# Linear attention with memories and a mixture of experts: values and logits projected in the routing, sorting in small steps, one-hots beside four tiles

## The chip, the cores and the metric

The kernel runs on one core of a Trainium2 chip. The core has a matrix engine (TensorE, PE in the profile; its weight loads are shown apart as PEld), a vector engine (VectorE, DVE), a scalar engine (ScalarE, ACT), a general engine (GpSimd, POOL) and an engine that here only issues transfers (SyncE, SP). Each works through its own queue of instructions in order and waits on semaphores for the others. TensorE writes its results to PSUM, of which this kernel uses eight banks of 512 fp32 values in each of 128 partitions; DVE and ACT read them from there. The metric is the device time of one execution in microseconds (us), and less is better. "Before" is the kernel as found, "after" the changed one.

## What is computed

The input x has 4096 tokens (4 sequences of 1024) of 256 channels. It is layer-normalised, and the result xn goes through an attention layer and a feed-forward layer; both outputs are added to x. Cut to what matters:

```python
xn = layernorm(x)
# attention, 16 heads of 16
q, k, v = (split(xn @ w.T) for w in (w_q, w_k, w_v))
sq, sk = elu(q) + 1, elu(k) + 1
out_coarse = (sq @ M) / (sq @ z)                    # M, z: four memories summed
out_fine = sum_m w[m] * (sq @ memory[m]) / (sq @ norm[m])
gprob = sigmoid(relu(coarse_repr @ eg_w1.T + eg_b1) @ eg_w2.T + eg_b2)
memory_output = gprob * out_fine + (1 - gprob) * out_coarse
local_output = causal_linear_attention(q, k, v)      # chunks of 128 tokens, running state
attn = (gate * memory_output + (1 - gate) * local_output) @ w_o.T
# experts: 8, each token goes to its best 2
scores = softmax(xn @ gate_weight.T)
cw = normalised weights of the two largest scores, else 0
y = sum_e cw[e] * (silu(xn @ w_gate[e].T) * (xn @ w_up[e].T)) @ w_down[e].T
y += (silu(xn @ sw_gate.T) * (xn @ sw_up.T)) @ sw_down.T     # shared expert
out = x + attn + y
```

The weights w[m] are a softmax over the memories of the mean of sq @ norm[m] over a sequence, so a whole sequence's queries have to be known before its first memory output.

## The kernel before, in words

All arithmetic is fp32. Tokens are handled in 32 tiles of 128, and in 8 blocks of four tiles. Python lists of units, each with a weight, are merged in proportion (`mix`) or cut into parts of equal weight (`split`), and their functions are called in that order (`run`); the schedule is manual, so each engine's queue holds its instructions just as the functions are called. What decides the time is therefore where in the lists a unit stands, and on which buffers it has to wait.

*The routing.* For each block: x is loaded (`load_x`), DVE makes the statistics (`statistics`; POOL takes the inverse root for two blocks together), ACT and DVE normalise in place (`normalize`, three tiles on ACT, one on DVE), SP writes the normalised block to the array xns in DRAM, TensorE transposes it (`transpose_x`, L334, copied to xnT by ACT), and `logits` multiplies xnT with a 128-column strip of the joined weights wvg to get 8 logits a token (L348). Six blocks of x fit; blocks 6 and 7 are loaded into the buffers of 0 and 1 once those are written to xns. Route of the first half and the queries of the first two blocks (L550) stand between the last blocks.

*The sorting.* `route` finds each token's two largest logits, `sort` counts by a matmul with a triangle of ones (pp), `slots` turns the counts into places, `shift_logits` and `weights` make the weights of the chosen experts, `owners` says which expert owns which of 71 slots of 128 places. Each is a run of short DVE instructions. Then 22 batches of at most three one-hots (a batch covers three of 64 columns of choices) invert the list: `invert` makes the one-hots on DVE (L499, L503) and two products on POOL (held, L510), `add_slots` adds them up by matmul into one bank (found, L518). `inverted` reads the slots' tokens (islot) and weights from it. These steps are mixed with the first block's keys, values and shared expert and the first two attention rounds.

*Attention rounds.* A round (`attention_round`) takes one tile through scores (L658, into quad), masks (DVE, L665), memories (L770, quad again), weights of the memories (L780 to L785), fine parts (L799), local output (pn, L684), the way back (pb, L700 and L706, read by DVE L714 to L718), the running state (pu, L750) and, one and two tiles later, the gate (`gate_hidden` L830, `gate_out` L840) and the output (po). Beside the first 28 rounds run the projections of later blocks: keys, values (`values`, L578), queries, shared gate and up (L856, L871).

*Experts.* From round 2 to round 29 (`first_round`, `last_round`) the 71 slots are spread evenly: gather 128 tokens from xns (`fetch`, POOL; SP loads the owner's weights), transpose (pxg, L959), gate and up (phe, L968), transpose (pTe, L982), down (pye, L991), and an indirect transfer that adds to the array sums in DRAM (`put`, L1000). The last four rounds add the parts up and write the output.

*PSUM.* quad takes four banks for the whole kernel; every other matmul takes its bank from a ring of four (`bank`, pool ps_r). A bank is given out anew when its last reader is through, and which bank that is has been settled when the program is built.

Of the kernel before, what the change touches and what calls it, by code (L numbers as in the profile page):

```python
# [8 lines left out]
FP = mybir.dt.float32  # L9
# [5 lines left out]
P = 128  # L15
# [7 lines left out]
def linear_attention_moe_kernel(  # L23
# [51 lines left out]
    AHEAD = 6  # L75
# [10 lines left out]
    big = ctx.enter_context(tc.tile_pool(name="big", bufs=AHEAD))  # L86
# [3 lines left out]
    ps_q = ctx.enter_context(tc.tile_pool(name="ps_q", bufs=1, space=bass.MemoryType.PSUM))  # L90
# [6 lines left out]

    quad = ps_q.tile([P, NG, 512], FP, tag="quad", name="quad")

# [4 lines left out]
    def load_x(blk):  # L104
        xb = big.tile([P, NT, H], FP, tag="tok", name=f"x_{blk}", bufs=AHEAD)
        nc.sync.dma_start(
            xb, x[blk * TB : (blk + 1) * TB, :].rearrange("(n p) h -> p n h", p=P)
        )
        st["x", blk] = xb

    for blk in range(AHEAD):
        load_x(blk)
# [18 lines left out]
    b1 = const.tile([HID, 1], FP, tag="b1", name="b1")  # L131
    nc.scalar.dma_start(b1, eg_b1)
    w2 = const.tile([HID, 1], FP, tag="w2", name="w2")
    nc.scalar.dma_start(w2, eg_w2)
# [23 lines left out]
    neghalf = const.tile([P, 2, NT], FP, tag="neghalf", name="neghalf")  # L158
# [129 lines left out]
    def statistics(blk):  # L288

        xb = st["x", blk]  # L290
        if blk % 2 == 0:
            st["mv"] = small.tile([P, 2, NT, 2], FP, tag="mv", name=f"mv_{blk}", bufs=3)
            st["rstd"] = small.tile([P, 2, NT], FP, tag="rstd", name=f"rstd_{blk}", bufs=3)
        mv, rstd = st["mv"], st["rstd"]
        for i in range(NT):
            stats = small.tile([P, 6], FP, tag="stats", name=f"stats_{blk}_{i}")
            nc.vector.bn_stats(stats, xb[:, i, :])
            nc.vector.bn_aggr(mv[:, blk % 2, i, :], stats)
        if blk % 2:
            nc.vector.tensor_scalar(rstd, mv[:, :, :, 1], LN_EPS, None, ALU.add)  # L300
            nc.gpsimd.tensor_tensor(rstd, rstd, neghalf, ALU.pow)
        st["norm", blk] = mv[:, blk % 2], rstd[:, blk % 2]

    def normalize(blk):
# [9 lines left out]
        nc.vector.tensor_scalar(  # L314
            xb[:, NT - 1, :], xb[:, NT - 1, :], mv[:, NT - 1, 0:1], rstd[:, NT - 1 : NT],
            ALU.subtract, ALU.mult,
        )
        for i in range(NT - 1):
# [7 lines left out]
        if blk + AHEAD < NBLK:  # L326
            load_x(blk + AHEAD)

# [13 lines left out]
    def logits(blk):  # L342

        xnT = st["xnT", blk]
        pl = bank(f"pl_{blk}").rearrange("p (i e) -> p i e", i=NT)
        for i in range(NT):
            for k in range(NC):
                nc.tensor.matmul(  # L348
                    pl[:, i, :], xnT[:, k, i * P : (i + 1) * P], wvg[:, k, H + E - P : H + E],
                    start=(k == 0), stop=(k == NC - 1),  # L350
                )
        nc.scalar.copy(lgs[:, blk * NT : (blk + 1) * NT, :], pl[:, :, P - E :])

    def route(half):
# [12 lines left out]
        def first_largest(v, best, m, name):  # L367

            nc.vector.tensor_tensor(m, v, spread(best), ALU.is_equal)
            nc.vector.tensor_mul(m, m, first[:, None, :].to_broadcast(sh))  # L370
            at = t2(name + "_at")
            nc.vector.tensor_reduce(at, m, AX.X, ALU.max)
            nc.vector.tensor_tensor(m, m, spread(at), ALU.is_equal)

# [3 lines left out]
        first_largest(lg, best, m1, "m1")  # L378
# [4 lines left out]
        first_largest(rest, low, m2, "m2")  # L383
        st["best", half] = best

    def shift_logits():
# [8 lines left out]
        nc.scalar.activation(gatew, gatew, AF.Exp)  # L395

    def weights():
# [4 lines left out]
        nc.vector.reciprocal(tot, tot)  # L402
        nc.vector.tensor_mul(gatew, gatew, tot[:, :, None].to_broadcast(sh))
        two = st["two"]
        both = tmp.tile([P, 2, NTT, E], FP, tag="h", name="chosen", bufs=2 * NF)
        nc.vector.tensor_mul(both, picks, gatew[:, None].to_broadcast([P, 2, NTT, E]))
        nc.vector.tensor_reduce(two, both.rearrange("p r i e -> p (r i) e"), AX.X, ALU.add)
        nc.vector.tensor_add(tot, two[:, :NTT], two[:, NTT:])
# [3 lines left out]
        nc.vector.tensor_mul(t2, t2, tot[:, None, :].to_broadcast([P, 2, NTT]))  # L412

    def sort():
# [5 lines left out]
        nc.vector.tensor_add(both, pick[0], pick[1])  # L420
        pp = bank("pp").rearrange("p (w i e) -> p w i e", w=2, e=E)
# [5 lines left out]
        st["pp"] = pp  # L427

    def slots():
        work, pp = st.pop("work"), st.pop("pp")  # L430

        cnt = work[:, 1].rearrange("p (e i) u -> p e (i u)", e=E)
        nc.vector.tensor_copy(cnt, pp[:, 0].rearrange("p i e -> p e i"))
        upto = work[:, 2].rearrange("p (e i) u -> p e (i u)", e=E)
# [3 lines left out]
        )  # L438

# [12 lines left out]
        st["ends"] = ends  # L452
        nc.vector.tensor_sub(wholef, ends, wholef)
        nc.vector.tensor_sub(upto, upto, cnt)
        nc.vector.tensor_add(upto, upto, wholef[:, :, None].to_broadcast([P, E, NTT]))
        place = work[:, 3]
        nc.vector.tensor_add(place, pp[:, 1], upto.rearrange("p e i -> p i e"))
        both = work[:, 0:2]
        nc.vector.tensor_mul(both, picks, place[:, None].to_broadcast([P, 2, NTT, E]))
        slot = small.tile([P, 2 * NTT], FP, tag="slot", name="slot", bufs=1)  # L460
        nc.vector.tensor_reduce(slot, both.rearrange("p r i e -> p (r i) e"), AX.X, ALU.add)

# [6 lines left out]
        st["lohi"] = lohi  # L469

    def owners():
# [10 lines left out]
        )  # L482
        ownf = small.tile([P, NST], FP, tag="ownf", name="ownf", bufs=1)
        nc.vector.tensor_reduce(ownf, own_e, AX.X, ALU.add)
        nc.vector.tensor_scalar(owner, ownf, float(E - 1), float(F), ALU.min, ALU.mult)

    def invert(lo):
# [21 lines left out]
        for v, what in enumerate((token, two)):  # L509
            nc.gpsimd.tensor_mul(  # L510
                held[:, :, v], tiles, what[:, some, None].to_broadcast([P, n, NST])
            )
        st["one hot", lo] = places, held
# [23 lines left out]
    def project(blk, w, c, is_q):  # L537
# [18 lines left out]
        nc.scalar.activation(ex, ex, AF.Exp, scale=-1.0)  # L556
        if is_q:
            nc.vector.scalar_tensor_tensor(  # L558
                st[name, blk][:, c, :], pq, 0.0, ex, ALU.max, ALU.add,
                accum_out=st["qs", blk][:, c : c + 1],  # L560
            )
        else:
            nc.vector.scalar_tensor_tensor(  # L563
                st[name, blk][:, c, :], pq, 0.0, ex, ALU.max, ALU.add
            )

    def values(blk, i):
        xnT = st["xnT", blk]
        if i == 0:
            wide = att.tile([P, NT, NH * D1 + CW - D1], FP, tag="va", name=f"va_{blk}")  # L570
            nc.gpsimd.memset(wide[:, :, NH * D1 :], 0.0)
            va = wide[:, :, : NH * D1].rearrange("p i (h k) -> p i h k", k=D1)
            nc.gpsimd.memset(va[:, :, :, HD:D1], 1.0)
            st["va", blk] = va
            st["wide", blk] = wide
        pv = bank(f"pv_{blk}_{i}")
        for k in range(NC):
            nc.tensor.matmul(  # L578
                pv[:, :H], xnT[:, k, i * P : (i + 1) * P], wvg[:, k, :H],
                start=(k == 0), stop=(k == NC - 1),  # L580
            )
        nc.scalar.copy(
            st["va", blk][:, i, :, :HD],
            pv[:, :H].rearrange("p (h k) -> p h k", k=HD),
        )
# [623 lines left out]
```

## Time and profile before

| what | value |
|---|---|
| median of 3 runs | 777.4 us (773.6 to 777.79) |
| the profiled execution's own time | 782.79 us |
| its span (first to last instruction) | 781.1 us |
| busy in the span: PE, PEld, DVE, ACT, POOL | 700.7, 491.0, 426.1, 273.8, 400.3 us |
| last logits of the routing start | 55.8 us |
| first expert slot's transpose starts | 155.6 us |
| rounds 2, 4, 28 and 30 start (first scores) | 156.2, 201.3, 703.0, 733.0 us |
| mean granted TensorE clock | 0.956 of full |

Engines are busy side by side, so their times don't add up to the span. A group of instructions is written as line, engine, operation, output<-input by the program's names, shapes and count, then busy time, mean length in ns, the engine's idle time just before, and what ended that. In a list of waits stand the engine, its line, what it waited for, the sum in us, how often, and the longest. The line of 40 digits cuts the span into equal slices of 19.5 us and gives the busy share of each in tenths. Idle time of an engine counts only where nothing else is late.

### The profile page before, as it was taken

How to read it: one execution, taken by the hardware profiler on the slowest of the kernel's cores; microseconds unless marked ns; L12 is line 12 of the kernel's file. 1: busy time of each engine (PE TensorE's matmuls, PEld its weight loads, DVE VectorE, ACT ScalarE, POOL GpSimd, SP SyncE). 2: the span in 40 equal slices, each digit the busy share in tenths (PEclk: the TensorE clock that was granted, in tenths of full speed). 3: DMA queues.
4: the chain of work that ended last, by engine and by line, in shares of the span. 5: the costliest groups of instructions: out<-in, count | busy, mean ns of one | idle time of the engine just before them, and what ended most of it. 6: DMA issues, size and time to landing. Idle time of an engine off the chain costs nothing.

```text
span 781.1 us, 14630 instructions
## 1 busy us (share of the span) xinstructions
PE 700.7 (90%) x5268; PEld 491.0 (63%) x5268; DVE 426.1 (55%) x1084; ACT 273.8 (35%) x707; POOL 400.3 (51%) x441
## 2 busy tenths in 40 slices
PE   1798579499999999999999999999999999999965
PEld 0675356366676666666667667666766667767653
DVE  6536857445446744455536644554457555655553
ACT  2563002123443333433443343433443344334300
POOL 3100366506555656464546555556545646657576
PEclk9899689889999999999999999999999999999976
DMA  9554000234343453344444443443443444454285
GB/s 283 183 178 134 1 0 1 59 107 97 84 117 85 90 118 84 86 106 94 97 111 92 103 104 84 93 113 84 97 104 85 107 101 103 108 123 99 29 261 171
DMA packets 86373, 81.48 MB, mean 104 GB/s; under 512 B 7437, under 2 KB 83901, under 8 KB 86173
## 3 DMA queue, kind: packets, MB, share of 16 engines
q1 hardware_dynamic: 69661, 59.64, 26.5%
q0 software_dynamic: 13632, 18.62, 14.3%
q10 hardware_dynamic: 3008, 2.28, 0.9%
q8 instruction: 42, 0.69, 0.4%
q14 instruction: 30, 0.25, 0.1%
HBM read 62.56 MB, written 22.15 MB: 108 GB/s over the span
## 4 chain that ended last, share of the span: by engine, by line
PE 76%; DVE 7%; DMA 5%; POOL 4%; ACT 3%; issue 3%; SPq 0%; POOLq 0%; DVEq 0%; ACTq 0%
PE phe L968 12%; PE pye L991 8%; PE po L895 5%; PE psu L871 5%; PE pg L856 5%; PE quad L658 4%; PE pn L684 4%; PE po L899 3%; PE pv L578 3%; PE pq L550 3%; PE pk L550 3%; PE quad L770 3%; PE pxg L959 2%; PE pTe L982 2%; PE ph L830 2%
## 5 line engine op out<-in xcount | busy, mean ns | idle before, releaser
L1000 POOL DMA_INDIRECT sums<-y,islot x71 | 112.7, 1588 | 81.0 <-DMA sums<-y,islot 29.9
L792 POOL TENSOR_TENSOR cg<-coarse,gates 128x256 f32<-128x256 f32 x32 | 23.7, 742 | 165.1 <-DVE coarse L785 164.9
L968 PE MATMUL phe<-wgu,xgT 128*128 128x352 f32 x284 | 100.9, 478 | 1.1 <-ACT hTe L984 0.9
L665 DVE TENSOR_TENSOR sT<-quad,causal 128x512 f32<-128x512 f32 x128 | 80.2, 682 | 14.3 <-PE pk L736 6.5
L933 POOL DMA_INDIRECT xg<-xns,islot x71 | 71.3, 1005 | 15.9 <-issue 8.8
L991 PE MATMUL pye<-wdn,hTe 88*128 88x256 f32 x284 | 76.6, 392 | 1.8 <-ACT oT L822 1.0
L968 PEld LDWEIGHTS phe<-wgu,xgT 128*128 128x128 f32 x284 | 49.9, 191 | 25.3 <-issue 5.3
L810 POOL TENSOR_TENSOR fm<-fm 128x512 f32<-128x512 f32 x32 | 43.6, 1363 | 36.5 <-DVE prob L843 23.1
L974 DVE SCALAR_TENSOR_TENSOR the<-the,phe 128x176 f32<-128x176 f32 x71 | 23.8, 335 | 69.6 <-ACT the L973 66.8
L991 PEld LDWEIGHTS pye<-wdn,hTe 88*128 88x128 f32 x284 | 49.5, 189 | 15.1 <-issue 5.5
L995 ACT ACTIVATE y<-pye,wslot 128x256 f32<-128x256 f32 x71 | 33.6, 473 | 58.6 <-PE pye L991 55.7
L895 PE MATMUL po<-wd,h 128*128 128x256 f32 (+1 forms) x192 | 49.2, 394 | 0.0
L973 ACT ACTIVATE the<-phe 128x176 f32<-128x176 f32 x71 | 22.5, 318 | 74.5 <-PE phe L968 72.5
L871 PE MATMUL psu<-xnT,wu 128*128 128x512 f32 (+1 forms) x96 | 47.6, 620 | 0.0
L856 PE MATMUL pg<-xnT,wg 128*128 128x512 f32 (+1 forms) x96 | 47.0, 613 | 0.7 <-ACT nT L691 0.7
L799 DVE TENSOR_TENSOR fm<-quad,rw 128x512 f32<-128x512 f32 x64 | 42.0, 682 | 0.0
L863 DVE SCALAR_TENSOR_TENSOR th<-th,pg 128x512 f32<-128x512 f32 (+1 forms) x24 | 16.4, 684 | 43.8 <-ACT th L862 39.6
L876 DVE SCALAR_TENSOR_TENSOR h<-th,psu 128x512 f32<-128x512 f32 (+1 forms) x24 | 16.5, 686 | 42.9 <-PE psu L871 42.2
L961 ACT COPY xgT<-pxg 128x256 f32<-128x256 f32 x71 | 26.5, 373 | 37.1 <-PE pxg L959 18.3
L895 PEld LDWEIGHTS po<-wd,h 128*128 128x128 f32 (+1 forms) x192 | 36.1, 200 | 4.3
L558 DVE SCALAR_TENSOR_TENSOR sqT<-pq,eq 128x512 f32<-128x512 f32 x16 | 11.1, 692 | 50.8 <-ACT eq L556 50.7
L563 DVE SCALAR_TENSOR_TENSOR skT<-pk,ek 128x512 f32<-128x512 f32 x16 | 11.1, 691 | 49.8 <-ACT ek L556 47.1
(195 smaller groups left out, 1510.2 us busy)
## 6 DMA issues: line engine op xcount, KB each, us to landing
wgu<-in_w_gate_dram SPq DMA_DIRECT2D x71, 176.0 KB
wgu<-in_w_up_dram SPq DMA_DIRECT2D x71, 176.0 KB
wdn<-in_w_down_dram SPq DMA_DIRECT2D x71, 176.0 KB
x<-in_x_dram SPq DMA_DIRECT2D x8, 512.0 KB
xns<-x SPq DMA_DIRECT2D x8, 512.0 KB
sums<-in_x_dram SPq DMA_DIRECT2D x8, 512.0 KB
part<-sums SPq DMA_DIRECT2D x14, 256.0 KB
out_dram<-acc SPq DMA_DIRECT2D x14, 256.0 KB
```

The costliest lines, as they stand in the source:

```text
L550: nc.tensor.matmul(pq, w[:, k, c * P : (c + 1) * P], xnT[:, k, :], start=(k == 0), stop=(k == NC - 1),)
L665: nc.vector.tensor_mul(sT, quad[:, g, :].rearrange("p (c t) -> p c t", t=P), causal[:, None, :].to_broadcast([P, NC * 2, P]),)
L799: nc.vector.tensor_mul(fm[:, c].rearrange("p g m (r k) -> p g (m r) k", k=HD), quad[:, :, c * KM + KX + KN : (c + 1) * KM].rearrange("p g ...
L810: nc.gpsimd.tensor_add(fm[:, :, 0:2, :], fm[:, :, 0:2, :], fm[:, :, 2:4, :])
L856: nc.tensor.matmul(pg[:n, :], wg[:, k, f * P : f * P + n], xnT[:, k, :], start=(k == 0), stop=(k == NC - 1),)
L871: nc.tensor.matmul(pu[:n, :], wu[:, k, f * P : f * P + n], xnT[:, k, :], start=(k == 0), stop=(k == NC - 1),)
L895: nc.tensor.matmul(po[:, :H], st["h", blk, f][:k, tok], wd[:k, f, :], start=(f == 0), stop=False)
L933: nc.gpsimd.indirect_dma_start(out=xg, out_offset=None, in_=xns, in_offset=bass.IndirectOffsetOnAxis(ap=islot[:, j : j + 1], axis=0),)
L968: nc.tensor.matmul(ph[:, : 2 * F], xgT[:, k, :], wgu[:, k].rearrange("p g f -> p (g f)"), start=(k == 0), stop=(k == NC - 1),)
L991: nc.tensor.matmul(py[:, :H], hT[:, f, :], wdn[:, f, :], start=(f == 0), stop=(f == 1))
L995: nc.scalar.activation(y, py[:, :H], AF.Copy, scale=wslot[:, j : j + 1])
L1000: nc.gpsimd.indirect_dma_start(out=sums, out_offset=bass.IndirectOffsetOnAxis(ap=islot[:, j : j + 1], axis=0), in_=st.pop(("y", j)), in_of ...
```

## The change

- **Values and logits in the routing.** All eight blocks of x are loaded at once. A new `values(blk, pair)` multiplies two tiles with all 264 columns of wvg, so that a tile's values and logits come from one pair of matmuls; `logits` is gone, and so are the values from the projections of every block. The results lie in two banks at a time of a pool of their own (ps_v, two buffers, the four banks that quad gets afterwards). ACT copies the values over the block's own x, which has been written to xns by then, DVE copies the logits, POOL sets the ones and zeros beside them. The order of the routing is a string, written out by hand; the queries of the first two blocks are no longer in it.
- **Normalising and statistics.** Block 0 gets its inverse root alone, the others in pairs (1, 2), (3, 4), (5, 6), and 7 alone; two tiles are scaled on DVE and two on ACT.
- **Sorting in steps.** `route`, `sort` (with `slots` in it), `shift_logits`, `weights` and `owners` become one generator; 32 steps of it are mixed with the queries of blocks 0 to 2, keys of 0 and 1 and the shared expert of 0.
- **Units in two halves.** The DVE end of a projection (`projected`, `shared_hidden`, and the first DVE step of the shared gate) is called one unit later (`late`). This holds for all later projections too.
- **One-hots beside four tiles.** The 22 batches run beside rounds 0 to 3 with shared(1), their matmuls two batches behind; three short ACT activations take one of POOL's two products. The experts start at round 4 instead of 2, with the first two fetches at the end of the lists.
- **The gate.** The hidden layer comes out with tokens in partitions (cT is the loaded operand, w1 streams 64 columns); bias, relu and the product with w2 are two DVE instructions, and the matmul pz and ACT's relu are gone.

```diff
-    big = ctx.enter_context(tc.tile_pool(name="big", bufs=AHEAD))
+    big = ctx.enter_context(tc.tile_pool(name="big", bufs=NBLK))
-    ps_q = ctx.enter_context(tc.tile_pool(name="ps_q", bufs=1, space=bass.MemoryType.PSUM))
...
-    for blk in range(AHEAD):
+        wide = big.tile([P, NT, VW], FP, tag="tok", name=f"x_{blk}")
+        xb = wide[:, :, :H]
...
+    for blk in range(NBLK):
         load_x(blk)
...
-    def logits(blk):
...
+    def values(blk, pair):
+
+        xnT, wide = st["xnT", blk], st["wide", blk]
+        if pair == 0:
+            st["va", blk] = wide[:, :, : NH * D1].rearrange("p i (h k) -> p i h k", k=D1)
+        va = st["va", blk]
+        pv = ps_v.tile([P, 2, 512], FP, tag="v", name=f"pv_{blk}_{pair}")
+        for j in range(2):
+            i = 2 * pair + j
             for k in range(NC):
                 nc.tensor.matmul(
+                    pv[:, j, : H + E], xnT[:, k, i * P : (i + 1) * P], wvg[:, k, :],
                     start=(k == 0), stop=(k == NC - 1),
                 )
+        tiles = slice(2 * pair, 2 * pair + 2)
+        nc.scalar.copy(
+            va[:, tiles, :, :HD], pv[:, :, :H].rearrange("p i (h k) -> p i h k", k=HD)
+        )
+        first = blk * NT + 2 * pair
+        nc.vector.tensor_copy(lgs[:, first : first + 2, :], pv[:, :, H : H + E])
+        nc.gpsimd.memset(va[:, tiles, :, HD:D1], 1.0)
+        nc.gpsimd.memset(wide[:, tiles, NH * D1 :], 0.0)
...
         held = held[:, : n * 2 * NST].rearrange("p (n v s) -> p n v s", v=2, s=NST)
-        for v, what in enumerate((token, two)):
-            nc.gpsimd.tensor_mul(
-                held[:, :, v], tiles, what[:, some, None].to_broadcast([P, n, NST])
+        for k in range(n):
+            nc.scalar.activation(
+                held[:, k, 0], tiles[:, k], AF.Copy, scale=token[:, lo + k : lo + k + 1]
             )
+        nc.gpsimd.tensor_mul(
+            held[:, :, 1], tiles, two[:, some, None].to_broadcast([P, n, NST])
+        )
...
+        st["e" + what, blk, c] = pq, ex
+
+    def projected(blk, c, is_q):
+        what = "q" if is_q else "k"
+        pq, ex = st.pop(("e" + what, blk, c))
+        dst = st[f"s{what}T", blk][:, c, :]
...
-                ph[:HID, :P], w1[:, c, :], cT[:, c, :], start=(c == 0), stop=(c == NC - 1)
-            )
-        h1 = tmp.tile([HID, P], FP, tag="h1", name=f"h1_{n}")
-        nc.scalar.activation(h1, ph[:HID, :P], AF.Relu, bias=b1)
-        st["h1", n] = h1
+                ph[:, :HID], cT[:, c, :], w1[:, c, :], start=(c == 0), stop=(c == NC - 1)
+            )
+        h1 = tmp.tile([P, HID], FP, tag="h1", name=f"h1_{n}")
+        nc.vector.tensor_add(h1, ph[:, :HID], b1)
+        z = small.tile([P, 1], FP, tag="z", name=f"z_{n}")
+        nc.vector.scalar_tensor_tensor(h1, h1, 0.0, w2, ALU.max, ALU.mult, accum_out=z)
...
-        pz = bank(f"pz_{n}")
-        nc.tensor.matmul(pz[:, :1], st.pop(("h1", n)), w2, start=True, stop=True)
...
-    first_round, last_round = 2, 30
+    first_round, last_round = 4, 30
...
+    def late(pairs):
+
+        units = [pairs[0][0]]
+        for (_, b), (a, _) in zip(pairs, pairs[1:]):
+            units += [a, b]
+        return units + [pairs[-1][1]]
...
-        units = [(1, fetch, 0), (1, fetch, 1), (128, expert_in, 0)]
+        units = [(1000, lambda: None), (128, expert_in, 0)]
...
+    ahead = "S0 S1 masks N0 T0 S2 S3 N1 N2 V0 T1 T2 S4 memories V1 S5 N3 N4 V2 T3 T4 S6 gates V3 S7"
+    ahead += " N5 N6 V4 living T5 T6 N7 V5 route V6 T7 V7"
...
+    with tc.tile_pool(name="ps_v", bufs=2, space=bass.MemoryType.PSUM) as ps_v:
...
+    def sorting():
+        yield from route(1)
+        yield from sort()
+        yield from shift_logits()
+        yield from weights()
+        yield from owners()
+
+    first_pairs = queries(0) + queries(1) + keys(0) + shared(0) + keys(1) + queries(2)
+    start = [u for u in late(first_pairs) if u]
+    start.insert(9, (64, mean_queries, 0))
+    start += [(64, batch_weights, 0), (32, odd_keys, 0)]
+    run(mix(steps(sorting(), 32, 1000), start))
...
+    beside = [[u for u in late(shared(1)) if u]] + [projections(blk) for blk in range(2, NBLK)]
...
     for k, lo in enumerate(batches):
+        lists += [(400, invert, lo)]
+        lists += [(768, add_slots, batches[k - 2])] if k > 1 else []
+    lists += [(768, add_slots, lo) for lo in batches[-2:]]
+    lists += [(64, inverted), (10, fetch, 0), (10, fetch, 1)]
+    lists = split(lists, first_round)
+    for n in range(first_round):
+        run(mix(rounds[n], beside[n], lists[n]))
```

## The prediction

> **What bounds the kernel now.** I read the page first (parts 1, 2 and 4), then the busy times by stretch, the waits of TensorE, and the order of time at the front. The page:
>
> ```profile
> PE 700.7 (90%) x5268; PEld 491.0 (63%) x5268; DVE 426.1 (55%) x1084; ACT 273.8 (35%) x707; POOL 400.3 (51%) x441
> PE   1798579499999999999999999999999999999965
> PEclk9899689889999999999999999999999999999976
> PE 76%; DVE 7%; DMA 5%; POOL 4%; ACT 3%; issue 3%; SPq 0%; POOLq 0%; DVEq 0%; ACTq 0%
> ```
>
> TensorE carries 76% of the chain and is full from slice 9 on; only the first eight slices (156 us) have holes. By stretch (columns: busy PE, PEld, DVE, ACT, POOL, then clock, DMA share, GB/s):
>
> ```profile
> 58.00:97.00 39.00, 26.79 (x147) 16.84 (x145) 30.12 (x86) 6.68 (x15) 6.89 (x10) 0.79 0.23 73
> 97.00:114.00 17.00, 11.85 (x60) 8.95 (x56) 8.88 (x19) 1.58 (x3) 11.06 (x15) 0.87 0.00 0
> 114.00:148.00 34.00, 29.57 (x217) 21.90 (x215) 23.94 (x52) 8.64 (x18) 20.76 (x34) 0.95 0.00 1
> 148.00:156.00 8.00, 0.39 (x2) 0.29 (x2) 1.98 (x4) 0.00 (x0) 4.62 (x5) 0.58 0.46 131
> 201.00:733.00 532.00, 520.40 (x4078) 360.43 (x4076) 291.69 (x707) 208.88 (x558) 296.45 (x297) 1.00 0.44 98
> ```
>
> Sorting and one-hots (58 to 148) leave TensorE idle for 22 us and at a lower clock; the first gather costs 8 more. The 26 rounds from 201 to 733 are full: 11.6 us idle in 532. The waits of TensorE say on what:
>
> ```profile
> PE pt L334 <- ACT x L319: 19.9, 4, 16.0
> PE found L518 <- POOL held L510: 11.2, 6, 3.7
> PE pxg L959 <- DMA xg<-xns,islot: 9.4, 1, 9.4
> PE pcT L820 <- ACT oT L822: 1.5, 3, 1.0
> ```
>
> The first three stand at the front. The last is of the kind that returns below: a transpose that waits for another tile's copy, which can only be for its PSUM bank. Two groups that the change removes (matmul ends are modelled, so starts count for prices):
>
> ```profile
> L348 PE MATMUL pl<-wvg,xnT 128*128 128x128 f32 x128 | 18.9, 311 | 0.0
> L840 PE MATMUL pz<-w,h 64*128 64x1 f32 x64 | 12.1, 257 | 0.7 <-ACT h L834 0.7
> ```
>
> **What the Trainium skill says.** Of the PSUM, quad has four banks here and all else four. "Perfetto Trace Analysis", Matmuls: rotate matmul groups through banks so that the evacuation of one overlaps the next; Optimization Strategy: a gap that repeats on the engine that should be full can mean too little PSUM. The trace agrees only in small: 10 us of such waits in the 26 rounds. "SBUF — State Buffer", Who interferes with whom: a tensor_tensor with two SBUF inputs contends with GpSimd's reads. It agrees: L503 took 0.55 us with POOL idle (110.41) and 0.89 with POOL busy (111.93). "TensorE: Matmul & The Clock Gate", Part 1: the clock falls after an idle window; the trace has 0.79 in the stretch with long holes and 1.00 in the full one.
>
> **The change part by part.**
>
> *Removed from TensorE.* Logits: 16 matmuls, 1.78 us a block by the chain of waits, x 8 = 14.2. The values' matmuls widen from 256 to 264 columns: 8/256 of 0.87 us x 32 tiles = 0.9. Gate: ph to the next start 0.58 us (321.53 to 322.11), pz 0.31 (325.39 to 325.70). The new ph loads cT 128 wide and streams 64 columns; not in the trace: between 0.22 (two transposes of that load, half the matmuls) and 0.58. I take 0.47, so 0.42 a tile, 13.4 in 32. DVE gains an add and a multiply with accumulator, about 0.5 us a tile, ACT loses L834 (0.36); neither is full.
>
> *Routing.* Values of all tiles (32 x 0.87 to 0.97 us) come here, the first two blocks' queries (6.9 us) leave. ACT cannot start sooner: its load issues end at 13.75 and the table load at 15.03, as before. New is a wait in ACT's queue: V0's copy overwrites x of block 0, so it waits for xns 0 to be read out. That write, issued near 16.3, took 4.4 us before; now x 6 and 7 (1 MB at the 273 GB/s of the first 19 us, 3.8 us) lie ahead of it in SP's queue: it lands near 24. Behind the copy on ACT stand the copies of T1 and T2; on DVE, whose logits copy follows ACT's, S4 and the norms. From there I walk the written order with the trace's durations (statistics of a block 2.1 us, two scaled tiles 1.05 on ACT, transposes 1.1 a block, their copies 1.1, values 3.5 and copies 1.2, route 3.6): V1 copied at 31, N3 and N4 at 35.5, V2 36.7, V3 42, N5 and N6 47, V4 48, V5 54, V6 57, V7's matmuls end at 62. Before, this point was 57.6 with the queries done.
>
> *Sorting between projections.* TensorE: ten projections and six shared units at 1.72 = 27.5, pp and pr 1.5. DVE: route 1 3.6, the sorting rows 74.47 to 80.4 with L420 6.6, shift, weights and owners 6.0, sixteen unit ends of 0.69 = 11, mean queries 0.6, batch weights 2.5: 30. They interlock, because a projection keeps its bank until one unit later and pp has another: about 96 for the first attention round.
>
> *Rounds 0 to 3 with the lists.* TensorE: attention 26, shared(1) 10.3, found 22 x 0.75 = 16.5: 53. DVE: attention rows (L665 2.7, L780 to L785 1.7, L799 1.4, L714 to L718 1.2, L756 0.4, L843 and L845 1.1, new gate 0.5) 9.0 x 4 less 1.5 = 34.5; one-hots 22 at 0.92 (POOL idle) to 1.5, I take 1.15 = 25; shared 4.1, inverted 0.7: 64. POOL's half of held goes to ACT (64 short activations at some 0.25 us = 16), so POOL (34) stops being the bound and DVE is. It waits 2 to 3 us a round for ph, pb and pu: 64 + 10 = 74, end at 170. The first gather: islot 1.7 us after the last pu, then 5 as before (151.22 to 155.61), against scores and a projection of 3.4 us: 3 to 4 us lost. So round 4 starts near 175, against 201.3 before, but with no expert slot done instead of five.
>
> *From round 4 on.* Before it took 781.1 - 201.3 = 579.8. Now: values of blocks 2 to 7 out, 24 x 0.9 = -21.6; gate 29 x 0.42 = -12.2; 71 slots in 26 rounds instead of 65.9, 5.1 x 2.7 us (pxg, phe, pTe, pye) = +13.7. Leaves 559.7.
>
> *What is late next: banks.* A projection's bank is now held until the next unit beside the attention, 4 to 8 us on, instead of some 3. One of four banks, two at times, is out of rotation. In the built order of the expert rounds, 142 of 543 bank reuses come one or two allocations after the last use of that bank; before, 16 of 620. Evacuations, matched one by one in the trace (end of last matmul to end of last reader, medians): pxg 0.47, pye 0.51, pTe 0.55, pn 0.65, phe 1.10, pu 1.12, pb 1.92. Eleven reuses at distance one cost the whole of it, 0.6 = 7; eleven pb to pu with phe's 1.25 between, 0.8 = 9; eight pb to others 0.8 = 6; fourteen after pu 0.4 = 5; of the other hundred, a short transpose between leaves 0.1 on average, 10. Sum 37. DVE no longer stands waiting for L556, which lay ahead of pb's readers, so I take pb at its lower quarter, 1.5: 30 us (1.2 a round). Ends: 5, if engines with slack empty banks at their minimum, and 55, with mean delays instead of medians.
>
> Sum: 175 + 559.7 + 30 = 765 of span. The profiled execution took 782.8, 1.7 over its span and 5.4 over the median, so the median to expect is 765 + 1.7 - 5.4 = **761 us**.
>
> **The rivals.**
>
> *Bank waits don't bite* (chance 0.22). For it: ACT is 35% busy, and stalls of TensorE give the others time. Against it: a reuse at distance one has nothing to hide behind. 175 + 560 + 5, less 4: 736.
>
> *Bank waits eat it all, slower* (0.27). One mechanism: in the expert rounds TensorE waits for a bank over and over. It decides from 781 - 175 - 560 = 46 us, 1.8 us a round. For it: in before, the same count gives 4 to 7 us where the trace has 10, so queues lengthen evacuations; pb's upper quarter is 2.83. Against it: pauses of TensorE shorten those queues. At 60 us: 791.
>
> *The lists stay the bound* (0.11 for about no change). If DVE contends throughout (one-hots at 1.5 us, 8 us more) and waits 5 us a round, round 4 starts at 191 and the gain is gone: 777. For it: DVE was only half busy from 97 to 114; against it: that stretch waited for POOL.
>
> **How the numbers follow.** The likeliest case (0.40) has round 4 at 170 to 180 and bank waits of 20 to 40: its own range is 746 to 776. The rivals add 736 and 791 with some 5 around them; leaving a tenth out at each end gives 735 to 790. A measurement of this kernel tells about 0.5% from no change, 3.9 us. The first rival and all but a sliver of the main case are faster: 0.62; the third is the same, 0.11; slower 0.27.
>
> **What would show it.** Right: no L348 or pz group; first transposes still near 16; a wait of ACT's first values copy for the xns write; TensorE fuller and DVE near 85% before round 4; POOL no longer the releaser of found; fewer TensorE waits before 175; and in the 26 rounds new waits of pn, pu, pb, pxg and po for copies of other tiles, 30 us in sum, at clock 1.00. Wrong: those waits at 10 or less, or above 46; round 4 starting later than 185; a routing beyond 70 because writes and loads share the DMA engines worse than I worked out.

## The result, and the profile after

The changed kernel takes 784.5 us (median of 4, 783.7 to 786.0) where the kernel before takes 777.4 (773.6 to 777.8): a ratio of 1.0105, 95% interval 1.0075 to 1.0134. It is about 1% slower. In a later set of runs the same two took 793.9 and 780.3, a ratio of 1.0177 (1.0133 to 1.0221). The forecast was 761, faster; the time lies in its range of 735 to 790, on the wrong side of no change.

The two profiled executions have almost the same span, 781.1 before and 781.0 after. The one of before lies 5.4 us over its kernel's median and the one of after at its median, so in sum the differences below are some 5 us too small; in which stretch isn't known. What changed is where the time lies. Rounds are counted from the first scores of a round in the trace:

| stretch, us | before | after | difference |
|---|---|---|---|
| start to round 0 | 73.0 | 95.7 | +22.7 |
| rounds 0 to 3 | 128.3 | 78.2 | -50.1 |
| rounds 4 to 29 | 531.7 | 554.2 | +22.5 |
| round 30 to the end | 48.1 | 53.0 | +4.9 |

The front won 27.4 us, as planned; the 26 expert rounds and the tail gave all of it back. The page's first two parts, of the changed kernel:

```profile
PE 677.8 (87%) x5076; PEld 468.1 (60%) x5076; DVE 455.2 (58%) x1205; ACT 273.7 (35%) x707; POOL 388.5 (50%) x436
PE   1789986887999998999999998999999998999665
PEclk9899988898999999999999999999999999999965
```

TensorE has 192 matmuls less and 23 us less of busy time, but its row, which was an unbroken run of nines from slice 9 on, now has eights in it. The clock is nearly as before (mean 0.958, before 0.956), but not in the rounds: 0.99 there in place of 1.00. What that costs is worked out further below. Busy times by stretch of the changed kernel (columns: length, busy PE, PEld, DVE, ACT, POOL with counts, clock, DMA share, GB/s), cut at the sorting, rounds 0 to 3, rounds 4 to 29 and the tail:

```profile
66.00:96.00 30.00, 29.66 (x82) 13.45 (x81) 24.07 (x67) 14.23 (x24) 0.00 (x0) 1.00 0.20 62
96.00:174.00 78.00, 63.18 (x574) 48.45 (x571) 59.36 (x136) 28.52 (x93) 33.56 (x42) 0.87 0.03 8
174.00:728.00 554.00, 512.98 (x3990) 348.12 (x3990) 315.50 (x800) 199.11 (x527) 307.63 (x297) 0.99 0.43 103
728.00:781.00 53.00, 30.45 (x250) 23.86 (x248) 24.51 (x56) 5.89 (x16) 33.89 (x33) 0.71 0.54 166
```

In the third line TensorE is idle for 41 us of 554; before, it was idle for 11.6 of 532. The waits of TensorE in rounds 4 to 29 of the changed kernel say on what:

```profile
PE pu L771 <- DVE loc L739: 9.1, 10, 1.2
PE pb L721 <- ACT nT L712: 3.5, 10, 0.4
PE pxg L986 <- DMA xg<-xns,islot: 3.4, 1, 3.4
PE pn L705 <- ACT y L1022: 3.2, 6, 0.6
PE pxg L986 <- PE pu L771: 2.1, 6, 0.7
PE po L922 <- ACT xgT L988: 1.4, 3, 0.5
```

Two of them are data: pb transposes the nT that ACT has just copied, and the first slot waits for its gather. One, pxg behind pu, is shown as a wait for TensorE's own last matmul, and the trace doesn't tell more. The other three can only be banks. The running state pu needs x and sk, not loc; but loc is computed from pb, so pu waits until pb's bank is empty. In the same way pn waits for the copy of another slot's pye, and po for the copy of pxg. A piece of the rounds shows it in order of time (start, length, instruction; in brackets the idle time before it and who ended it):

```profile
302.75 1.88 PE L877 MATMUL pg<-xnT,wg 128*128 128x512 f32 x4
...
306.84 0.63 PE L727 MATMUL pb<-state,sqT 128*128 128x136 f32 x4
307.31 1.03 PE L1018 MATMUL pye<-wdn,hTe 88*128 88x256 f32 x4
309.26 0.70 PE L771 MATMUL pu<-x,sk 128*128 128x136 f32 x4 [0.92 <-DVE loc L739]
...
310.57 1.45 PE L995 MATMUL phe<-wgu,xgT 128*128 128x352 f32 x4 [0.38 <-DVE state L777]
...
313.32 1.88 PE L891 MATMUL psu<-xnT,wu 128*128 128x512 f32 x4
```

The shared gate pg of 302.75 is read for the last time by a DVE step that is called behind psu, at 313. For ten microseconds the ring of four has three banks, and pb, pye and pu follow each other through them: pu waits 0.92 for pb's bank, phe 0.38 for pu's. Matched one by one over the 26 rounds, the median time from pg's last matmul to its last reader went from 1.35 to 9.8 us, that of psu from 0.72 to 9.8.

### The profile page after: what moved, and what is told of

Its sections match the earlier page's. It is cut to its first block, busy times and chain, and to the rows that moved or that the text cites. A ratio compares the mean times of both kernels' runs of the same rounds, so it can differ in the third digit from the quotient of the medians.

```text
span 781.0 us, 14363 instructions
## 1 busy us (share of the span) xinstructions
PE 677.8 (87%) x5076; PEld 468.1 (60%) x5076; DVE 455.2 (58%) x1205; ACT 273.7 (35%) x707; POOL 388.5 (50%) x436
## 5 line engine op out<-in xcount | busy, mean ns | idle before, releaser
L686 DVE TENSOR_TENSOR sT<-quad,causal 128x512 f32<-128x512 f32 x128 | 80.5, 682 | 11.1 <-PE quad L679 10.8
L995 PEld LDWEIGHTS phe<-wgu,xgT 128*128 128x128 f32 x284 | 50.1, 192 | 29.2 <-issue 6.7
L922 PE MATMUL po<-wd,h 128*128 128x256 f32 (+1 forms) x192 | 52.4, 414 | 2.6 <-ACT xgT L988 1.4
L1000 ACT ACTIVATE the<-phe 128x176 f32<-128x176 f32 x71 | 22.5, 317 | 77.3 <-PE phe L995 77.3
L548 POOL TENSOR_TENSOR held<-ones,two 128x213 f32<-128x213 f32 (+1 forms) x22 | 16.9, 766 | 59.6 <-DVE ones L534 59.6
L922 PEld LDWEIGHTS po<-wd,h 128*128 128x128 f32 (+1 forms) x192 | 38.3, 208 | 10.6 <-ACT xgT L988 2.2
L866 DVE SCALAR_TENSOR_TENSOR o<-diff,prob,loc 128x256 f32<-128x256 f32 x32 | 39.4, 1232 | 3.8 <-POOL fm L831 0.5
L705 PE MATMUL pn<-sT,x 128*32 128x128 f32 x1024 | 34.6, 276 | 4.4 <-ACT y L1022 3.2
L771 PE MATMUL pu<-x,sk 128*128 128x136 f32 x112 | 19.5, 297 | 20.6 <-DVE loc L739 14.6
```

Of the source, the lines that this page charges most:

```text
L686: nc.vector.tensor_mul(sT, quad[:, g, :].rearrange("p (c t) -> p c t", t=P), causal[:, None, :].to_broadcast([P, NC * 2, P]),)
L705: nc.tensor.matmul(pn[CW * r : CW * (r + 1), q, :], wide[:, i, first : first + CW], st["sT", h // 2][:, c * 2 + h % 2, :], start=True, sto ...
L866: nc.vector.scalar_tensor_tensor(o, st.pop(("diff", n)), prob, st.pop(("base", n)), ALU.mult, ALU.add)
L922: nc.tensor.matmul(po[:, :H], st["h", blk, f][:k, tok], wd[:k, f, :], start=(f == 0), stop=False)
L995: nc.tensor.matmul(ph[:, : 2 * F], xgT[:, k, :], wgu[:, k].rearrange("p g f -> p (g f)"), start=(k == 0), stop=(k == NC - 1),)
```

## The experiments

Theory H (held banks): the late DVE ends take banks out of the ring, and that is what the rounds lose. Its rivals were the denser slots, the gate's new DVE work, and the place of the late DVE steps in DVE's queue. The letters in the expectations are those of the rivals at the time: D in the third is density, D in the ninth and tenth is DVE's order. Kernels of one group ran on one chip: experiments 1 to 4, 5 to 8, and 9 to 12; the kernel before took 776.65, 782.16 and 780.30 there. So ratios are compared, and stretches of traces within a group where a few microseconds matter. The changed kernel's first measurement, 784.5, is in none of these groups. Where experiments 1 to 4 are set against it, a few microseconds prove little; experiment 12 has it beside its variants.

**1. The ends of blocks 2 to 7 directly behind their projections.**

```diff
-        units = late(pairs)
+        units = [u for pair in pairs for u in pair]
...
         nc.scalar.activation(th[:n], pg[:n], AF.Tanh, scale=0.5)
+        if blk > 1:
+            nc.vector.scalar_tensor_tensor(th[:n], th[:n], 1.0, pg[:n], ALU.add, ALU.mult)
...
```

> The changed kernel, but the DVE ends of the projections and of the shared expert of blocks 2 to 7 stand right behind their matmuls again, as in the kernel before; all else is as changed. Theory H (a held bank): the late ends keep one or two of four banks out of rotation, and that is what TensorE waits for from round 4 on. 27 instead of 142 of 543 bank reuses come within two allocations, so rounds 4 to 29 fall from 554 us by 25 to 40, and the whole from 784.5 to 745 to 760. Theory D (denser experts): the waits come from 71 slots in 26 rounds, whose steps hang on each other through ACT and DVE; rounds 4 to 29 stay at 548 or above, the whole at 778 or above. Theory G (the gate on DVE): its two new DVE instructions delay the readers of the banks; again no change, 778 or above.

Measured: 751.3 us, ratio 0.9677 (0.9636 to 0.9718). The busy line of its rounds 4 to 29:

```profile
173.00:695.00 522.00, 500.73 (x4000) 347.95 (x3998) 317.42 (x800) 198.51 (x528) 308.16 (x297) 0.99 0.47 109
```

The rounds shrank from 554.2 to 521.6, by 32.6 us, with the same instructions. Of pu, only 2 waits for loc are left in the whole execution, of 12. Note the busy PE: 500.73 here and 512.98 in the changed kernel, for ten matmuls fewer there. The ends of matmuls are modelled, so part of a wait is shown as busy; only starts show all of it.

**2. The other way round: the kernel before, with late ends for keys, queries and shared expert of blocks 2 to 7.**

```diff
+        if blk > 1:
+            pairs = [
+                ((1024, project, blk, wk, c, False, True), (64, projected, blk, c, False))
+                for c in range(NC)
+            ]
+            pairs += [((512, values, blk, i), None) for i in range(NT)]
...
+            units = late(pairs)
...
```

> The kernel before, with one part of the change alone: the DVE ends of keys, queries and shared expert of blocks 2 to 7 are called one unit later. Theory H: 101 instead of 16 of 620 bank reuses come within two allocations; rounds 4 to 29 rise from 532 us by 12 to 35, the whole from 777 to 790 to 812. Theories D and G: slots, gate and density are as before, so 532 plus or minus 4 and 774 to 781; DVE standing less behind ACT could even save a few us.

Measured: 803.9 us, ratio 1.0354 (1.0319 to 1.039). Rounds 4 to 29 went from 531.7 to 554.4. So this one part of the change, put alone into the old kernel, makes it 3.5% slower.

**3. Fewer slots a round: the experts spread over 28 rounds.**

```diff
-    first_round, last_round = 4, 30
+    first_round, last_round = 4, 32
```

> The changed kernel with the experts spread over rounds 4 to 31 instead of 4 to 29, so 2.54 slots a round as before instead of 2.73; the output's last sums fall into two rounds instead of four, so the end is longer and only rounds 4 to 27 are compared (522.9 us in the changed kernel). Theory H: the 4.7 slots fewer save their price of 2.77 us each, 13 us, so 507 to 513; the waits stay. Theory D: the waits go as well, 24 rounds of 20.45 less values (20) and gate (11): 460 to 495. Theory G: as H.

Measured once: 792.4 us. Rounds 4 to 27 went from 522.9 to 514.5. Over 28 rounds in place of 26 the slots are thinner, by 4.7 in these 24 rounds, which is 13 us at 2.77 a slot; 8.4 were won. From round 30 on, where there are slots now too, 15.5 were lost. Theory D, which had 460 to 495, is out; H's own range (507 to 513) was missed by 1.5.

**4. The changed kernel with the old gate.**

```diff
-                ph[:, :HID], cT[:, c, :], w1[:, c, :], start=(c == 0), stop=(c == NC - 1)
+                ph[:HID, :P], w1[:, c, :], cT[:, c, :], start=(c == 0), stop=(c == NC - 1)
             )
...
+        pz = bank(f"pz_{n}")
+        nc.tensor.matmul(pz[:, :1], st.pop(("h1", n)), w2, start=True, stop=True)
...
```

> The changed kernel with the old gate (w1 loaded, cT streamed, relu on ACT, the matmul pz). Theories H and D: the gate's price returns, 0.42 us a tile, and rounds 4 to 29 rise from 554 to 561 to 568, the whole from 784.5 to 792 to 800. Theory G: DVE loses 0.5 us a tile and its readers of banks come sooner; rounds 4 to 29 stay at 554 or fall by up to 20, the whole is 770 to 785.

Measured: 780.4 us, ratio 1.0047 (1.0033 to 1.006), below the changed kernel's 1.0105. H and D, which had 792 to 800, both missed this; the outcome is G's. The rounds take 555.9 with the old gate and 554.2 with the new one, although the new one has 11.8 us less of matmuls there (start to start: pz 9.2 and ph 14.9 with the old one, ph 12.3 with the new). TensorE's idle time in the rounds is 29.4 with the old gate and 41.0 with the new: what the gate saved turned into waiting. Whether G's reason is the right one, experiment 5 tests. The new gate also starts round 4 3.1 us later and makes the tail 2.8 us longer.

**5. Prompt ends and the old gate.** The edits of experiments 1 and 4 together.

> The version with prompt ends (751.3 us) with the gate of before: hidden layer with tokens in columns, relu on ACT, the matmul pz. Theory H (the gate's saving of 12 us on TensorE is real and was only eaten by bank waits, because the gate adds DVE work in front of evacuations): with banks free again the old gate costs its 12 us, 760 to 765 us, rounds 4 to 29 at 530 to 534 instead of 521.6. Rival G (the two DVE instructions of the new gate cost TensorE as much as they save, whatever the banks): 747 to 753 us, rounds 4 to 29 at 518 to 523.

Measured: 759.9 us, ratio 0.974 (0.9689 to 0.9791). With free banks the gate is worth something in the rounds: 535.8 with the old one, 526.7 with the new one and prompt ends in experiment 6, on the same chip. That is 9.1 of the 10.9 us forecast for 26 rounds. H holds for the rounds, where G had no change; in the total the intervals of the two overlap (0.974 and 0.9684), since the new gate is again slower outside them: round 4 starts at 170.4 with the old gate and at 172.7 to 176.3 with the new one in experiments 1, 6 and 7.

**6 and 7. Prompt ends in rounds 0 to 3 too, and everywhere.**

```diff
-    beside = [[u for u in late(shared(1)) if u]] + [projections(blk) for blk in range(2, NBLK)]
+    beside = [[u for pair in shared(1) for u in pair if u]] + [projections(blk) for blk in range(2, NBLK)]
...
-    start = [u for u in late(first_pairs) if u]
+    start = [u for pair in first_pairs for u in pair if u]
...
```

The first line is experiment 6; both are 7. The first DVE step of the shared gate moves with them.

> The version with prompt ends (751.3 us), and the ends prompt in shared(1) beside rounds 0 to 3 too, so that no bank is held there beside found and the attention. Theory H (a held bank costs wherever four banks are shared): rounds 0 to 3, 78.3 us there, shorten by 2 to 6 us, total 746 to 750. Rival L (in rounds 0 to 3 DVE is the bound, and a prompt end only puts DVE in front of an evacuation that isn't ready): no change or up to 3 us longer, 751 to 754.

> As the version with prompt ends from round 0, and the ends prompt in the sorting stretch too, where six steps of sorting stand between projections. Theory H (only the held bank matters): the stretch from V7 (66 us) to the first scores (94.8) gets shorter by 2 to 4 us, total 743 to 748. Rival L (an end called at once makes DVE's queue wait for ACT's exponential, and the short sorting steps queue behind it): 4 to 10 us longer, 754 to 762.

Measured: 757.2 us, ratio 0.9684 (0.9653 to 0.9715), and 759.5, ratio 0.9736 (0.9692 to 0.9779). H expected gains; the ratios show none over the 0.9677 of experiment 1. Rounds 0 to 3 took 79.8 and 77.9 us, against 78.3 in experiment 1. The sorting stretch, from V7's last matmul to the first scores, took 30.4 us in seven and 29.2 in six: 1.2 longer with prompt ends, where H had 2 to 4 shorter and L 4 to 10 longer. Seven's runs lay between 754.5 and 764.4, so its total settles nothing finer. So the held banks cost in the expert rounds, and not measurably in the front. Why not is open. In the changed kernel's sorting stretch TensorE is as full as in the rounds (29.66 of 30 us), and in rounds 0 to 3 it is 81% busy and DVE 76%, so a full DVE is not shown to be the reason.

**8. Late ends only for the shared expert of blocks 2 to 7.**

```diff
-        units = late(pairs)
+        n = len(pairs) - 2 * NF
+        units = [u for pair in pairs[:n] for u in pair] + late(pairs[n:])
```

> The changed kernel with prompt ends for keys and queries of blocks 2 to 7, late ones kept for the shared expert there. It has 74 of 543 bank reuses within two allocations; the changed kernel has 142, that with prompt ends 27. Theory H, in proportion to the count of such reuses: 41% of the 32.6 us between the two, rounds 4 to 29 at about 535 (530 to 540), total 761 to 768. Rival: a held bank costs only where the next unit is far (all kinds alike, 18 of 40 late units are the shared expert's), the cost follows the number of late units: 45%, nearly the same; or the cost sits in keys and queries alone: 521 to 526, total 751 to 756; or in the shared expert alone: 550 to 555, total 780 to 785.

Measured: 769.0 us, ratio 0.983 (0.98 to 0.9861). The rounds take 541.9, against 526.7 in experiment 6 on the same chip: 15.2 us. Total and rounds lie just above H's ranges. The changed kernel isn't in this group: 15.2 is 47% of the 32.6 us that experiment 1 gave back, and 38% of the 39.9 between the changed kernel and prompt ends in the last group. So the cost is spread over both kinds, as the count of near reuses (41%) and that of late units (45%) both have it, and these two can't be told apart here; the rivals that put all of it on one kind fall.

**9. Prompt ends, and one bank of the ring occupied from round 4 to round 29.**

```diff
+    hold = bank("hold")
+    nc.tensor.matmul(hold[:, :P], ident, ident, start=True, stop=True)
     side = split(experts(), last_round - first_round)
...
+    held = small.tile([P, 1], FP, tag="held1", name="held1", bufs=1)
+    nc.vector.tensor_copy(held, hold[:, :1])
```

> The version with prompt ends (751.3 us), and from round 4 to round 29 one bank of the ring held by a dummy: one small matmul into it before round 4, one read of it after round 29. No DVE instruction of the rounds is moved, three banks are left, 200 of 543 reuses come within two allocations (27 with prompt ends, 142 in the changed kernel). Theory H (the late ends cost because they hold banks): by the count of reuses, 173/115 of 32.6 us = +49 us, rounds 4 to 29 at 560 to 580, total 790 to 808. Rival D (the late ends cost because their DVE steps stand in the way of others): three banks are nearly enough, +0 to +12 us, rounds 4 to 29 at 522 to 534.

**10. Late ends that read a copy, so that the bank is free.**

```diff
+        if "rounds" in st:
+            dst = st[name, blk][:, c, :]
+            nc.scalar.copy(dst, pq)
+            pq = dst
         st["e" + what, blk, c] = pq, ex
...
+            h = tmp.tile([P, TB], FP, tag="h", name=f"h_{blk}_{f}", bufs=2 * NF)
+            nc.scalar.copy(h[:n], pu[:n])
+            pu = h
...
```

> The changed kernel with all 40 late DVE ends of blocks 2 to 7 left where they are, but reading a copy: ACT copies the projection from its bank to where the result goes (22 keys and queries, 18 shared up, about 0.6 us each on ACT), and the bank is free at once; the gate's first DVE step is prompt. 12 of 543 reuses within two allocations. Theory H: bank waits go as with prompt ends, rounds 4 to 29 at 516 to 528, total 745 to 758. Rival D: the DVE order is that of the changed kernel but for 18 steps, so at least two thirds of the 32.6 us stay: rounds 4 to 29 at 543 to 556, total 773 to 787.

**11 and 12. Prompt ends and the changed kernel again, beside these two.**

> The version with prompt ends again, beside the changed kernel on one chip. Theory H: 32 to 33 us below the changed kernel (ratio to before near 0.968). No rival.

> The changed kernel itself, beside the other three on one chip. Expected as measured before: ratio to the kernel before 1.0075 to 1.0134. If the time of the kernel before moves by chip and the ratio with it, the ratio comes out below 1.005.

Measured, experiments 9 to 12 in this order: 809.8 us, ratio 1.0389 (1.0354 to 1.0425); 752.8, ratio 0.9657 (0.9629 to 0.9686); 753.2, ratio 0.9653 (0.9627 to 0.968); 793.9, ratio 1.0177 (1.0133 to 1.0221). The last is outside what was expected: on this chip the late ends cost 40.7 us, not 33. The total of experiment 9 is 2 us above H's range, its rounds are inside. The lines of the rounds, in the same order:

```profile
176.00:754.00 578.00, 520.49 (x3996) 349.05 (x4000) 313.24 (x795) 199.94 (x528) 307.13 (x295) 0.99 0.42 98
175.00:699.00 524.00, 501.56 (x3992) 349.30 (x3991) 317.69 (x800) 217.17 (x567) 319.19 (x297) 0.99 0.46 109
174.00:699.00 525.00, 499.56 (x3991) 346.75 (x3991) 313.69 (x799) 197.67 (x526) 307.99 (x296) 1.00 0.46 108
176.00:741.00 565.00, 514.93 (x3991) 347.51 (x3990) 307.78 (x799) 198.47 (x526) 308.48 (x296) 0.99 0.43 101
```

This decides between the bank and DVE's order. Experiment 9 moves no DVE instruction in the rounds and takes a bank: the rounds go from 525.2 (experiment 11) to 577.4, +52.2, where H said +49 and the rival at most +12. Experiment 10 leaves all 40 late DVE ends where the change put them and frees the banks, at the price of 40 copies on ACT (23 us in sum); only the shared gate's first step, which would need a copy of its own, is prompt there. Its rounds take 524.0, where the changed kernel beside it takes 565.1: all of the loss is gone, where the rival kept two thirds of it. Its waits in the rounds show no pu behind loc any more, and the data wait of pb is on top:

```profile
PE pb L725 <- ACT nT L716: 10.0, 13, 1.7
PE pxg L999 <- DMA xg<-xns,islot: 3.4, 1, 3.4
PE pcT L845 <- ACT skT L597: 2.7, 4, 1.2
```

Where the time goes, as sums from start to next start over the 26 rounds, in us:

| unit | changed | 1: prompt | 9: bank taken | 10: copied |
|---|---|---|---|---|
| expert slots (pxg, phe, pTe, pye) | 230.5 | 207.9 | 238.3 | 213.3 |
| pu | 17.4 | 15.8 | 23.5 | 10.8 |
| pcT and poT | 17.5 | 12.8 | 25.6 | 12.4 |
| near reuses (one or two allocations) of 543 | 142 | 27 | 200 | 12 |

The near reuses are counted in the order of the built program. A sum from start to next start holds the wait of whatever comes next. So most of the loss lies behind the slots' matmuls, but it isn't the slots alone that wait: pu, in the list further up with 9.1 us, often follows one. And the price of a near reuse comes out much the same in each pair: 32.6/115 = 0.28 us (39.9/115 = 0.35 on the other chip) for the changed kernel against prompt ends, 22.7/85 = 0.27 in experiment 2 (101 near reuses of 620, 16 before), 15.2/47 = 0.32 in experiment 8 (74 of 543), 52.2/173 = 0.30 in experiment 9.

That agrees with what the prediction took from the Trainium skill, "Perfetto Trace Analysis", Optimization Strategy, on gaps that repeat: here too little PSUM is what makes them. The late ends are worth 33 to 40 us of some 525, a bank that is gone for good 52.

## Why the prediction was wrong

The sum of spans was 175 + 559.7 + 30 = 765, and 781.0 came. The mechanism that the prediction named is the one that was found. What failed are terms of its sum, all on one side. The step from span to median was put at -3.7 us and came out at +3.5; the tail, which no step priced, grew by 4.9 where the gate alone was to shorten it by 1.3; the bank waits, put at 30, were some 35; the clock behind the first gather, put at nothing, cost 3.0; and the front with that gather came 2.3 later than 175. By its own steps:

- *Routing.* Right within a few microseconds. First transposes at 16.23. ACT's first values copy waits 6.1 us for the xns write, as foreseen, and starts at 26.94 (the write was to land near 24). V7's matmuls end at 66.3 instead of 62.
- *Sorting between projections.* Forecast 96 for the first round, came 95.7. That is luck: the routing ended 4 us late and the sorting took 4 us less than worked out (TensorE is busy for 29.66 of 30 us).
- *Rounds 0 to 3.* Forecast "near 175" with the gather's loss in it; round 4's scores stand at 173.9 and the gather's wait of 3.4 comes behind them, together 2.3 more. DVE is 76% busy (85% forecast), POOL releases found no more, and TensorE is idle for 40 us of the first 174, where it was idle for 51 before. The third rival, round 4 at 191 with the lists still the bound, is out.
- *Removed from TensorE.* Values: 22.5 us gone from the rounds (21.6 forecast). Gate: 12.2 (10.9 forecast for 26 rounds). Slots: 71 instead of some 66, as forecast. Without bank waits the steps give 531.7 - 21.6 - 10.9 + 13.7 = 512.9 for the 26 rounds.
- *The clock behind the gather.* No step priced it. About 2 us into the gather's wait the clock falls to half for 6.8 us, and a phe there takes 0.59 us an instruction where the median of the rounds is 0.30:

```profile
180.00:187.00 7.00, 5.40 (x13) 3.65 (x14) 0.67 (x2) 1.06 (x3) 1.93 (x3) 0.52 0.34 95
182.68 2.71 PE L995 MATMUL phe<-wgu,xgT 128*128 128x352 f32 x4
317.07 1.45 PE L995 MATMUL phe<-wgu,xgT 128*128 128x352 f32 x4
```

Against the medians of the same instructions this costs 3.0 us. Before, the gather stood ahead of these rounds, and their clock was 1.00 throughout.
- *Banks.* Right in kind, with pu, pn and po in the list of waits as it said, and too small: "I take pb at its lower quarter, 1.5: 30 us". The rounds took 554.2, 41.3 over 512.9. Of that, 3.4 is the gather and 3.0 the clock, leaving some 35, or 0.28 for each of the 126 near reuses more than before; 30 would be 0.24. Its count at medians, 37, was nearer than the 30 that came of the correction for pb, although pb did empty faster, as the correction assumed (median 1.92 before, 1.57 after). Banks were also held longer than it said: "4 to 8 us on" was 9.8 in the median. Experiment 1 gives back 32.6 of the 35; on another chip experiments 11 and 10 give back 39.9 and 41.1. The gate's saving is not independent of the banks either (experiments 4 and 5): where TensorE waited for banks, 1.7 us of it were left, and 9.1 with free ones.
- *The tail.* No step priced it. It was to shrink by 1.3 us and grew by 4.9. The old gate alone takes 2.8 off (experiment 4); on the chain that ends last in the tail the new gate's product L857 stands with 1.9 us. The transfers of the last slots land 11.8 us behind the start of round 30, before 8.9; that the denser slots make this is argued and wasn't tested.
- *From span to median.* The prediction took 5.4 us off because the profiled execution of before lay that far over its median. Of the changed kernel the profiled execution (784.1) lies at the median (784.5), which is 3.5 over its span. So the step had -3.7 where 3.5 came, 7.2 us. Where in the execution of before its extra time lay isn't known; if it lay in the stretches that the change replaced, it had no place in the new sum.
- *One reading.* At 110.41 POOL was idle only when L503 started; its product came 0.23 us later, at 110.64, and took 1.77 us, where the one at 103.81 took 0.53. So that pair of L503 has DVE slow where POOL had begun first, and POOL slow where DVE had; neither row shows L503 with POOL idle throughout.

The errors add up: 2.3 for the front with the gather, 3.0 for the clock, 5 for banks, 6.2 for the tail, 7.2 for the offset make 23.7, and 784.5 - 761 is 23.5. All have one sign, and none alone would have turned the forecast, which had 16 us to spare. The outcome is that of the second rival, "bank waits eat it all", but not by its own line: it wanted 46 us of bank waits, and some 35 came, inside the 20 to 40 of the likeliest case. What came over 559.7 behind round 4, 607.1 - 559.7 = 47.4, holds the gather, the clock and the tail as well. And moving the late DVE calls of blocks 2 to 7 back by one unit turns the same change into a gain of 3.2% (experiment 1).

## What to carry to other kernels

When an evacuation is moved behind other work, count what it holds. In the expert rounds here, each bank reuse that came to stand within two allocations cost 0.27 to 0.35 us of TensorE, in four pairs of kernels; in the front no such cost was to be seen. To keep the late call, read the bank into SBUF first on the engine that has room (ACT was 35% busy): that gave the same time as calling it at once. And a saving on the engine that is waiting for buffers was hardly one here until the buffers were free. Last, several small terms that were left out or rounded down did more to this forecast than its largest unknown.

## What the runs showed of the hardware

- Busy time of TensorE is not its work: the same matmuls of the rounds count as 499.6 to 501.6 us busy with free banks, 513.0 and 514.9 with late ends and 520.5 with a bank taken.
- The gate's hidden layer streams half the columns (64 instead of 128) and took 105 to 118 ns an instruction from start to start instead of 143 to 145, not half.
- The new gate's DVE part takes 0.87 us a tile (0.21, 0.58 and 0.08 for reading the accumulator), where 0.5 was expected. The tile's view in the changed kernel (min/median/max ns):

```profile
L855 DVE TENSOR_TENSOR h<-ph,b x32: 211/214/225, 127.1 to 768.7; 128x64 f32<-128x64 f32 x32
L857 DVE SCALAR_TENSOR_TENSOR h<-h,w x32: 224/718/1129, 127.3 to 768.9; 128x64 f32<-128x64 f32 x32
```

The first reads PSUM and hardly varies. The second reads SBUF twice, on the same 64 columns: about 0.22 us where POOL's product cg ended as it began, about 0.72 where cg ran beside it for 0.64. That is the conflict that the prediction took from the Trainium skill, "SBUF — State Buffer", Who interferes with whom; the trace agrees, but no run took POOL's work away to show it.
- The cost of the held banks was not the same everywhere: 33 us between the first measurement of the changed kernel and experiment 1, 40 between experiments 12 and 11 on another chip, while the kernel before stood at 777 and 780. Why is open.
